# Attention stage of a two-layer model: weight loads in quarters, gathers on three units, two joins and one turn moved

## The chip, the cores and the metric

The kernel runs on one core of a Trainium2 chip. Its time is the device time in microseconds (us) of one execution. The core has five engines that run their own instruction queues: TensorE (PE in the profile; PEld is its weight load), VectorE (DVE), ScalarE (ACT), GpSimd (POOL) and SyncE (SP). SP only issues transfers here; 16 DMA engines carry them out. Engines wait for each other through semaphores.

## The reference

Four blocks, each added to a residual x of 4 x 512 rows of 512 numbers: a state-space block on a context, a mixture of experts, a cross-attention on the same context, and a ternary feed-forward. All in f32. The change touches the third block and the order of work around it:

```
x = x + _L0_xattn_ref(ctx_1024, _layernorm(x), ...)
x = x + _L0_ffn_ref(_layernorm(x), ...)
x = x + _L1_xattn_ref(_layernorm(x), ctx_1024, L1_xattn_Wq, L1_xattn_Wk, L1_xattn_Wv, L1_xattn_Wo, L1_xattn_gq, L1_xattn_gk)
x = x + _L1_ffn_ref(_layernorm(x), L1_ffn_w1, L1_ffn_w2)

def _L1_xattn_ref(hidden_states, encoder_hidden_states, Wq, Wk, Wv, Wo, gq, gk):
    q = (hidden_states @ Wq).reshape(B, Sq, H, D)
    k = (encoder_hidden_states @ Wk).reshape(B, Skv, H, D)
    v = (encoder_hidden_states @ Wv).reshape(B, Skv, H, D)
    q = rmsnorm(q, gq)
    k = rmsnorm(k, gk)
    scores = jnp.einsum('bqhd,bkhd->bhqk', q, k) * scale
    attn = jax.nn.softmax(scores, axis=-1)
    out = jnp.einsum('bhqk,bkhd->bqhd', attn, v)
    return out.reshape(B, Sq, H * D) @ Wo
```

Here there are 4 batches of 512 queries and 512 keys, 16 heads of 128.

## The kernel before

The last function, `attend`, holds the attention, and between its steps the end of the expert block (gathers of expert rows and their sum), the layer norms and the feed-forward of the batch before. Keys and values were computed earlier and lie in device memory.

**Tiling.** A *group* is four heads of one batch (16 groups, `groups`; 64 heads, `heads`). A head's 512 queries are taken in four *quarters* of 128 rows (`KB` is 4). One step of the main loop, a *unit* u = 4 n + i, belongs to quarter i of head n. Quarters go through five steps that are spread over units:

- `scores(n, i)`: one matmul into a PSUM bank (two banks), VectorE takes each row's maximum (L1958), ScalarE the exponential and the row's sum (L1961). The result, e, has three buffers.
- `weights(n, i)`, one unit later: VectorE's reciprocal (L1966) and scaling of e (L1967).
- The scaled quarter is turned, in one of two ways. `turn`: four transposes on TensorE into PSUM (`pet`, L2020) and a copy by ScalarE (L2021). Or by DMA: `split` takes the two 16-bit halves apart into `planes` (ScalarE L1985, GpSimd L1986), SP issues a DMA transpose (L1988) into `turned`, and two units later `join` copies the halves together into `eT` (VectorE L1995, ScalarE L1996). `by_dma` says which: from head 4 on the first three quarters go by DMA, and the fourth by TensorE; the last head goes by TensorE altogether.
- `values(n)`, at the third unit (i = 2) of head n + 1: four matmuls (`po`, L2027), once all four quarters are in `eT`.
- `project`: the product with Wo for one of the four row blocks (`px`, L2036), a group later.

The queries of the next group are projected meanwhile, one row block per head: `queries` (L1921) at i = 1, then ScalarE's square (L1924), `norm_q` at i = 2, `scale_q` at i = 3, and the turn of the normed queries, by DMA for the first three blocks (`split_q`, `join_q`), by TensorE for the fourth (`turn_q`). Groups 1 to 14 do this (56 heads); group 0's and group 1's queries are projected ahead of the loop, and group 15 has none to project.

**The order** is written out by hand. Each engine runs its instructions in program order, so a step that waits holds up everything behind it on its engine, and SP's queue holds the loads and the transposes of all heads in one line. In each unit the loop calls the steps of attention, then the list `front` (steps that begin with a matmul), then `weights` and `split`, then the list `back`. The steps that the change touches stand in the lists like this, with u the first unit of a head:

```
        if h == 0:
            put(back, u, load_q, j + 2)
            put(back, u + 1, load_o, b, g)
...
            for k in range(3):
                if 0 <= 3 * (at - 2) + k < NC * TOPK:
                    put(back, u + k, add, 1)
            if 0 <= 3 * (at - 1) < NC * TOPK:
                put(back, u + 2, fetch, min(3, NC * TOPK - 3 * (at - 1)))
```

`load_q` loads a group's 512 columns of Wq, `load_o` its 512 rows of Wo, 1 MB each, once per group. `fetch` issues gathers of one expert's row for 128 tokens each (`yg`, L1845, an indirect DMA issued by GpSimd, four buffers); `add` sums them into x on VectorE (L1853). In the first three batches heads 1 to 11 of the batch fetch.

**Queues around the steps.** On SP, one head's line is: transposes of quarters 0, 1 and 2, the loads of a later head's keys, key scales and values (`load_kv`), the transpose of the queries. On GpSimd, a head's line is: planes of quarters 0 and 1, two small steps of `norm_q` (L1932, L1933), the three gathers, planes of quarter 2, the scaling of a later head's keys (L1913), planes of the queries. The feed-forward's steps of the batch before stand between these from batch 1 on.

The last keys (batches 2 and 3) are still computed before the loop; `key_row` gives the buffers for their squares and for the keys, both from the seven buffers `oT`.

Of the kernel before, what the change touches and what calls it, by code (L numbers as in the profile page):

```python
# [17 lines left out]
F32 = mybir.dt.float32  # L18
# [12 lines left out]
P = 128  # L31
B, S, DM = 4, 512, 512
NT = B * S // P
NC = DM // P
# [4 lines left out]
E, TOPK, SEL, FI = 64, 8, 4, 192  # L39
# [19 lines left out]
HG = 4  # L59
# [1126 lines left out]
class Keys:  # L1186
# [4 lines left out]
    KB = S // P  # L1191
# [622 lines left out]
def attend(ctx, cm, x_all, w, kv, y_dram, wk, pos, tern, late, ctx_k, wk_k, out):  # L1814
# [5 lines left out]
    tc, nc = cm.tc, cm.nc  # L1820
    pool = {n: ctx.enter_context(tc.tile_pool(name=f"c_p{n}", bufs=n)) for n in (1, 2, 3, 4, 7)}
# [5 lines left out]
    W4 = HG * HD  # L1827
    KB = S // P
# [4 lines left out]
    heads = [(b, g, h) for b, g in groups for h in range(HG)]  # L1833
    xnTs, st = {}, {}
# [45 lines left out]
        nc.scalar.copy(xnTs[t], pt)  # L1880


    def load_q(j):
        if j < len(groups):
            b, g = groups[j]
            s = st[b, g] = {}
            s["Wq"] = pool[2].tile([P, NC, W4], F32, name="Wq")
            nc.sync.dma_start(s["Wq"], w["Wq"][:, g * W4:(g + 1) * W4].rearrange(
                "(c p) e -> p c e", p=P))

    def load_o(b, g):
        s = st[b, g]
        s["Wo"] = pool[2].tile([P, HG, DM], F32, name="Wo")
        nc.sync.dma_start(s["Wo"], w["Wo"][g * W4:(g + 1) * W4, :].rearrange("(h p) e -> p h e",
                                                                             p=P))

    def load_kv(n):
        if n < len(heads):
# [52 lines left out]
    def scores(n, i):  # L1951

        b, g, h = heads[n]
        pscore = psc.tile([P, S], F32, name="psc")
        nc.tensor.matmul(pscore, st[b, g]["qT"][:, h, i * P:(i + 1) * P], ks[n],  # L1955
                         start=True, stop=True)
        mx = small.tile([P, 1], F32, name="mx")
        nc.vector.tensor_reduce(mx, pscore, AX.X, ALU.max, negate=True)  # L1958
        e = pool[3].tile([P, S], F32, name="e")
        tot = small.tile([P, 1], F32, name="tot")  # L1960
        nc.scalar.activation(e, pscore, AF.Exp, bias=mx, accum_out=tot)  # L1961
        es[n, i] = e, tot

    def weights(n, i):
        e, tot = es[n, i]
        nc.vector.reciprocal(tot, tot)  # L1966
        nc.vector.tensor_scalar(e, e, tot, None, ALU.mult)  # L1967

    planes, turned = {}, {}

    def by_dma(n, i):
        if not HG <= n < len(heads) - 1:
            return False
        return i < 3

    def split(n, i):

        e, _ = es.pop((n, i))
        turned[n, i] = turn_planes(e[:, :])

    def turn_planes(e):

        halves = e.bitcast(I16).rearrange("p (s two) -> p two s", two=2)
        t = pool[2].tile([P, 2, S], I16, name="planes")
        nc.scalar.copy(t[:, 1], halves[:, 1])  # L1985
        nc.gpsimd.tensor_copy(t[:, 0], halves[:, 0])  # L1986
        out = pool[3].tile([P, 2 * KB, P], I16, name="turned")
        nc.sync.dma_start_transpose(out, t.rearrange("p two s -> p (two s)"))  # L1988
        return out

    def join_planes(out, t, i):

        out = out.bitcast(I16).rearrange("p k (s two) -> p two k s", two=2)
        at = slice(i * P, (i + 1) * P)
        nc.vector.tensor_copy(out[:, 1, :, at], t[:, KB:])  # L1995
        nc.scalar.copy(out[:, 0, :, at], t[:, 0:KB])  # L1996

    def join(n, i):

        if n not in eTs:  # L2000
            eTs[n] = pool[1].tile([P, KB, S], F32, name="eT")
        join_planes(eTs[n][:, :, :], turned.pop((n, i)), i)
# [11 lines left out]
    def turn(n, i):  # L2014
        if n not in eTs:
            eTs[n] = pool[1].tile([P, KB, S], F32, name="eT")
        e, _ = es.pop((n, i))
        pt = ptr.tile([P, KB, P], F32, name="pet", tag="pt")
        for kc in range(KB):
            nc.tensor.transpose(pt[:, kc, :], e[:, kc * P:(kc + 1) * P], cm.ident)  # L2020
        nc.scalar.copy(eTs[n][:, :, i * P:(i + 1) * P], pt)  # L2021

    def values(n):
        po = pav.tile([HD, S], F32, name="po")
        eT, v = eTs.pop(n), vs.pop(n)
        for kc in range(KB):
            nc.tensor.matmul(po, v[:, kc, :], eT[:, kc, :], start=kc == 0, stop=kc == KB - 1)  # L2027
        oTs[n] = pool[7].tile([HD, S], F32, name="oT")
        nc.scalar.copy(oTs[n], po)
# [122 lines left out]
    front, back = {}, {}  # L2152

    def put(where, u, f, *a):
        where.setdefault(u, []).append((f, *a))

    last = len(groups) - 1
    for n, (b, g, h) in enumerate(heads):
        j = n // HG
        u = n * KB  # L2160
        if j < last and j > 0:
            after = groups[j + 1]
            put(front, u + 1, queries, *after, h)
            put(back, u + 2, norm_q, *after)
            put(back, u + 3, scale_q, *after)
            if h < HG - 1:
                put(back, u + 4, split_q, *after, h)
                put(back, u + 6, join_q, *after, h)
        if j > 0:
            put(front, u + 4, project, j - 1, h)  # L2170
        if j < last and j > 0 and h == HG - 1:
            put(front, u + 4, turn_q, *groups[j + 1], h)
        if j > 0:
            put(back, u + 5, take_projected, j - 1, h)
        if h == 0:
            put(back, u, load_q, j + 2)
            put(back, u + 1, load_o, b, g)
        put(back, u + 3, load_kv, n + 3)
        put(back, u + 3, norm_k, n + 2)
        at = n % H  # L2180
        if b + 1 < B:
            for k in range(3):
                if 0 <= 3 * (at - 2) + k < NC * TOPK:
                    put(back, u + k, add, 1)
            if 0 <= 3 * (at - 1) < NC * TOPK:
                put(back, u + 2, fetch, min(3, NC * TOPK - 3 * (at - 1)))
            if at >= 11 and at < 15:
                t = (b + 1) * NC + at - 11
                put(back, u + 1, stats, t, "c")
                put(back, u + 3, normed, t, "c")  # L2190
                put(front, u + 4, turn_x, t)
        if b > 0 and h == 1:
            t = (b - 1) * NC + g
            put(back, u + 2, stats, t, "d")
            put(back, u + 4, ffn_x, t)
            put(back, u + 5, ffn_xq, t)
            put(front, u + 6, ffn_xT, t)

            put(front, u + 7, ffn_up, t, 0)
            put(front, u + 11, ffn_up, t, 1)  # L2200
            for k, at in enumerate((8, 9, 12, 12)):
                put(back, u + at, ffn_max, t, k)
            put(back, u + 12, ffn_h, t)
            for k in range(4):
                put(back, u + 13 + k // 2, ffn_hq, t, k)
            put(front, u + 14, ffn_hT, t, 0)
            put(front, u + 15, ffn_hT, t, 1)
            put(front, u + 15, ffn_down, t, 0)
            put(front, u + 19, ffn_down, t, 1)
            put(back, u + 20, ffn_y, t)  # L2210
            put(back, u + 20, store, t)

    def do(where, u):
        for f, *a in where.pop(u, []):
            f(*a)
# [5 lines left out]

    def key_row(n):

        return pool[7].tile([P, S], F32, name=f"k_{n}", tag="oT")

    def key_bank(shape, name):
        if name == "kpss":
            return pav.tile(shape, F32, name=name, tag="po")
        return psc.tile(shape, F32, name=name, tag="psc")

    keys = Keys(cm, w, kv, small, key_row, key_bank,
                lambda b: (ctx_k[b], 0), direct=ms)
    keys.wk = wk_k
# [13 lines left out]
    for n in range(NC * TOPK):  # L2247
        at = n % 16 - KB
        if n >= 16 and 0 <= at < KB:
            at = -1  # L2250
# [22 lines left out]
    for i in range(NC):  # L2273
# [3 lines left out]
        at = FRONT + i * WINDOW  # L2277
# [18 lines left out]
    for f, n, time in ((load_q, 0, 9.5), (load_kv, 0, 14.5), (load_q, 1, 17.5), (load_kv, 1, 44),  # L2296
                       (load_kv, 2, 50)):
        later(time, f, n)
# [17 lines left out]
    for *_, f, a in sorted(steps, key=lambda x: x[:2]):  # L2316
        f(*a)
    assert not left
    load_q(2)
    load_o(0, 0)  # L2320
    load_kv(3)
    put(back, KB * 3 + 4, last_norms)
# [3 lines left out]
    for u in range(KB, len(heads) * KB + 2):  # L2326
        n, i = divmod(u, KB)
        if n < len(heads):
            scores(n, i)
        if i == 2:  # L2330
            values(n - 1)
        if not by_dma(*divmod(u - 2, KB)):
            turn(*divmod(u - 2, KB))
        if by_dma(*divmod(u - 3, KB)):
            join(*divmod(u - 3, KB))
        do(front, u)
        if n < len(heads):
            weights(*divmod(u - 1, KB))
            if by_dma(*divmod(u - 1, KB)):
                split(*divmod(u - 1, KB))  # L2340
        do(back, u)
        if u == len(heads) * KB:
            weights(*divmod(u - 1, KB))
# [124 lines left out]
```

## Time and profile before

| | us |
|---|---|
| runs shown: median of 3 | 2537.57 |
| lowest and highest | 2534.87, 2537.62 |
| the profiled execution | 2537.26 |
| its span, first to last instruction | 2535.3 |
| TensorE busy in the span | 2367.0 |
| VectorE, ScalarE, GpSimd busy | 1585.2, 1362.9, 1333.4 |
| window 1470 to 2400: TensorE busy of 930 | 893.32 |
| window 2400 to 2535: TensorE busy of 135 | 112.03 |

The state-space block fills about the first 600 us, the experts run to about 1370, the attention with the feed-forward inside to about 2466, and the last batch's feed-forward ends the span. The profile comes from one execution. A line of its groups or waits names the source line (L1967 is line 1967 of the kernel), the engine, what is written and read, and how often. A "wait" is idle time of an engine in front of an instruction, with what ended it. "Granted clock" is the share of TensorE's clock that the chip let through in that stretch; "DMA share" is the mean busy share of the 16 DMA engines.

### The profile page before, as it was taken

The numbers are of one execution on the slowest core, as the hardware profiler recorded it, in microseconds if no ns is written. First come the engines' busy times: TensorE is split into PE (matmuls) and PEld (weight loads), VectorE is DVE, ScalarE is ACT, GpSimd is POOL, SyncE is SP. The second block draws the span as 40 slices with busy tenths as digits, with TensorE's granted clock in tenths as the row PEclk, the third lists the DMA queues.
The fourth block names the chain that finished last, engine by engine and source line by source line (L and its number), as shares of the span: only waits on it lengthen the run. The fifth ranks groups of instructions, "written<-read, shape, count | busy, mean of one in ns | idle before, by whom it ended". The sixth has DMA issues, their size and how long they took to land. (4 is left out here: it accounts for less than half of the span.)

```text
span 2535.3 us, 29085 instructions
## 1 busy us (share of the span) xinstructions
PE 2367.0 (93%) x9051; PEld 1289.9 (51%) x9051; DVE 1585.2 (63%) x2784; ACT 1362.9 (54%) x2554; POOL 1333.4 (53%) x1327
## 2 busy tenths in 40 slices
PE   6989899988999999999998988999999999999987
PEld 2555555655556566667664433444444444444443
DVE  6999998946332443344324565667776787666646
ACT  6777777755222222232323455666667666766753
POOL 7999999930443444444325344445553565333312
PEclk8999999989999999999998999999999999999999
DMA  5362636242766677899856467678876887666630
GB/s 207 96 217 79 224 109 209 96 162 99 232 213 206 204 231 235 282 314 340 269 186 217 151 171 176 168 172 192 191 172 151 191 198 179 144 142 136 139 77 21
DMA packets 445378, 456.17 MB, mean 180 GB/s; under 512 B 280756, under 2 KB 321796, under 8 KB 441121
## 3 DMA queue, kind: packets, MB, share of 16 engines
q1 hardware_dynamic: 401758, 297.86, 42.3%
q0 software_dynamic: 41408, 156.20, 20.0%
q8 instruction: 74, 1.21, 0.2%
q14 instruction: 88, 0.71, 0.1%
q10 hardware_dynamic: 2050, 0.18, 0.1%
HBM read 312.18 MB, written 79.82 MB: 155 GB/s over the span
## 5 line engine op out<-in xcount | busy, mean ns | idle before, releaser
L1315 PE MATMUL pg<-xT,wg 128*128 128x284 f32 (+12 forms) x1536 | 393.7, 400 | 1.8 <-ACT h L1326 0.7
L1986 POOL COPY planes<-e 128x512 int16<-128x512 int16 x177 | 117.0, 661 | 456.4 <-DVE e L1967 246.1
L1315 PEld LDWEIGHTS pg<-xT,wg 128*128 128x128 f32 x1536 | 278.6, 191 | 91.7 <-issue 41.8
L493 POOL TENSOR_TENSOR dBu<-bb,du 128x1024 f32<-128x1024 f32 x128 | 303.3, 2391 | 4.0 <-DVE dA L518 3.4
L1958 DVE TENSOR_REDUCE mx<-psc 128x1 f32<-128x512 f32 x256 | 175.9, 687 | 203.9 <-PE psc L1955 201.3
L1256 POOL DMA_INDIRECT xg<-xn_dram,tok x168 | 174.2, 1037 | 202.7 <-PE pt L1299 147.7
L1961 ACT ACTIVATE e<-psc,mx 128x512 f32<-128x512 f32 x256 | 176.4, 689 | 165.4 <-DVE mx L1958 160.6
L1955 PE MATMUL psc<-kT,qT 128*128 128x512 f32 x512 | 260.0, 594 | 0.2 <-ACT e L1961 0.2
L2027 PE MATMUL po<-eT,v 128*128 128x512 f32 x512 | 232.0, 596 | 13.8 <-ACT eT L1996 10.1
L1921 PE MATMUL pq<-Wq,xnT 128*128 128x512 f32 x512 | 233.9, 600 | 2.6 <-ACT xnT L1880 1.5
L2036 PE MATMUL px<-Wo,oT 128*128 128x512 f32 x512 | 230.9, 594 | 0.5 <-DVE qn L1939 0.5
L504 ACT ACTIVATE dA<-delta,negA 128x512 f32<-128x512 f32 x256 | 176.5, 695 | 52.0 <-DVE hc L519 31.6
L518 DVE TENSOR_TENSOR_SCAN dA<-dA,dBu 128x1024 f32<-128x1024 f32 x80 | 186.5, 2331 | 16.3 <-ACT dA L504 6.5
L1360 DVE COPY yo<-po 128x512 f32<-128x512 f32 x68 | 46.9, 691 | 197.9 <-PE po L1349 197.9
L2027 PEld LDWEIGHTS po<-eT,v 128*128 128x128 f32 x512 | 95.8, 190 | 141.7 <-issue 113.6
L2036 PEld LDWEIGHTS px<-Wo,oT 128*128 128x128 f32 x512 | 95.9, 190 | 123.7 <-issue 105.2
L524 PEld LDWEIGHTS yT<-ident,hc 128*128 128x128 f32 x1024 | 118.0, 143 | 78.5 <-issue 44.7
L1360 ACT COPY yo<-po 128x512 f32<-128x512 f32 (+3 forms) x64 | 37.5, 587 | 222.9 <-PE po L1349 215.9
L1256 POOL DMA_INDIRECT wd<-down,widx x64 | 62.9, 982 | 176.5 <-PE po L1349 163.1
L524 PE MATMUL yT<-ident,hc 128*128 128x128 f32 x1024 | 132.0, 276 | 20.7 <-DVE yg L558 9.7
L1967 DVE TENSOR_SCALAR e<-e,tot 128x512 f32<-128x512 f32 x256 | 141.3, 552 | 13.7
L1996 ACT COPY eT<-turned 128x512 int16<-128x512 int16 x177 | 135.6, 766 | 23.2 <-DMA turned<-planes 23.2
(367 smaller groups left out, 4613.0 us busy)
## 6 DMA issues: line engine op xcount, KB each, us to landing
y_dram<-yo SPq DMA_DIRECT2D x110, 256.0 KB
bb<-bc_dram SPq DMA_DIRECT2D x16, 1024.0 KB
cb<-bc_dram SPq DMA_DIRECT2D x16, 1024.0 KB
v_dram<-v SPq DMA_DIRECT2D x64, 256.0 KB
k_dram<-k_kT SPq DMA_DIRECT2D x64, 256.0 KB
Wq<-Wq SPq DMA_DIRECT2D x16, 1024.0 KB
kT<-k_dram SPq DMA_DIRECT2D x64, 256.0 KB
rk<-r_dram SPq DMA_DIRECT2D x64, 256.0 KB
```

What stands on the lines that cost most here:

```text
L493: nc.gpsimd.tensor_tensor(dBus[q], st[b]["bb"][i // 2][:, j:j + 2, :], st[b]["du"][c].unsqueeze(1).to_broadcast([P, 2, S]), ALU.mult)
L504: nc.scalar.activation(dAs[q][:, j, :], st[b]["delta"][c], AF.Exp, scale=negA[:, c, n:n + 1])
L518: nc.vector.tensor_tensor_scan(*flat, 0.0, ALU.mult, ALU.add)
L524: nc.tensor.matmul(yT[:, lc, :], t[:, lc * P:(lc + 1) * P], cm.ident, is_transpose=True, start=first and lc == 0, stop=last, skip_group_ch ...
L1256: nc.gpsimd.indirect_dma_start(out=t[0:n, :], out_offset=None, in_=table, in_offset=bass.IndirectOffsetOnAxis(ap=index, axis=0))
L1315: nc.tensor.matmul(pg[:, 0:n], s["wg"][:, c, m * P:(m + 1) * P], s["xT"][:, c, 0:n], start=c == 0, stop=c == NC - 1)
L1921: nc.tensor.matmul(pq.rearrange("p h d -> p (h d)"), xnTs[b * NC + i][:, c, :], s["Wq"][:, c, :], start=c == 0, stop=c == NC - 1)
L1955: nc.tensor.matmul(pscore, st[b, g]["qT"][:, h, i * P:(i + 1) * P], ks[n], start=True, stop=True)
L1958: nc.vector.tensor_reduce(mx, pscore, AX.X, ALU.max, negate=True)
L1961: nc.scalar.activation(e, pscore, AF.Exp, bias=mx, accum_out=tot)
L2027: nc.tensor.matmul(po, v[:, kc, :], eT[:, kc, :], start=kc == 0, stop=kc == KB - 1)
L2036: nc.tensor.matmul(px, oTs[j * HG + h][:, i * P:(i + 1) * P], st[b, g]["Wo"][:, h, :], start=h == 0, stop=h == HG - 1)
```

## The change

- Wq and Wo are loaded in four quarters of 256 KB, one in each head of a group, in place of one load of 1 MB at the group's first head.
- The three gathers of a head are issued at its first, second and fourth unit, one each, in place of all three at its third.
- Heads 60 to 62 turn their third quarter on TensorE.
- The joins of quarters 0 and 1 (at i = 3 and i = 0) stand behind `weights` and `split` of their unit; the join of quarter 2 (at i = 1) stays in front.
- The fourth quarter's turn (at i = 1) stands behind `front`, which holds the queries' projections.
- The squares of the last keys take their row from the two buffers `planes`.

```
-    def load_q(j):
+    def load_q(j, c0=0, c1=NC):
         if j < len(groups):
             b, g = groups[j]
-            s = st[b, g] = {}
-            s["Wq"] = pool[2].tile([P, NC, W4], F32, name="Wq")
-            nc.sync.dma_start(s["Wq"], w["Wq"][:, g * W4:(g + 1) * W4].rearrange(
-                "(c p) e -> p c e", p=P))
-
-    def load_o(b, g):
+            if c0 == 0:
+                st[b, g] = dict(Wq=pool[2].tile([P, NC, W4], F32, name="Wq"))
+            nc.sync.dma_start(st[b, g]["Wq"][:, c0:c1, :],
+                              w["Wq"][c0 * P:c1 * P, g * W4:(g + 1) * W4].rearrange(
+                                  "(c p) e -> p c e", p=P))
+
+    def load_o(b, g, h0=0, h1=HG):
         s = st[b, g]
-        s["Wo"] = pool[2].tile([P, HG, DM], F32, name="Wo")
-        nc.sync.dma_start(s["Wo"], w["Wo"][g * W4:(g + 1) * W4, :].rearrange("(h p) e -> p h e",
-                                                                             p=P))
+        if h0 == 0:
+            s["Wo"] = pool[2].tile([P, HG, DM], F32, name="Wo")
+        nc.sync.dma_start(s["Wo"][:, h0:h1, :],
+                          w["Wo"][g * W4 + h0 * P:g * W4 + h1 * P, :].rearrange(
+                              "(h p) e -> p h e", p=P))
...
         if not HG <= n < len(heads) - 1:
             return False
-        return i < 3
+        return i < (3 if n < len(heads) - HG else 2)
...
-        if h == 0:
-            put(back, u, load_q, j + 2)
-            put(back, u + 1, load_o, b, g)
+        if j > 0:
+            put(back, u, load_q, j + 2, h, h + 1)
+            put(back, u + 1, load_o, b, g, h, h + 1)
...
-            if 0 <= 3 * (at - 1) < NC * TOPK:
-                put(back, u + 2, fetch, min(3, NC * TOPK - 3 * (at - 1)))
+            for k in range(3):
+                if 0 <= 3 * (at - 1) + k < NC * TOPK:
+                    put(back, u + (0, 1, 3)[k], fetch, 1)
...
     def key_row(n):
 
+        if n == "sq":
+            return pool[2].tile([P, S], F32, name="k_sq", tag="planes")
         return pool[7].tile([P, S], F32, name=f"k_{n}", tag="oT")
...
-        if not by_dma(*divmod(u - 2, KB)):
-            turn(*divmod(u - 2, KB))
-        if by_dma(*divmod(u - 3, KB)):
-            join(*divmod(u - 3, KB))
+        before, landed = divmod(u - 2, KB), divmod(u - 3, KB)
+        if not by_dma(*before) and i != 1:
+            turn(*before)
+        if by_dma(*landed) and i == 1:
+            join(*landed)
         do(front, u)
+        if not by_dma(*before) and i == 1:
+            turn(*before)
         if n < len(heads):
             weights(*divmod(u - 1, KB))
             if by_dma(*divmod(u - 1, KB)):
                 split(*divmod(u - 1, KB))
+        if by_dma(*landed) and i != 1:
+            join(*landed)
         do(back, u)
```

## The prediction

> **What bounds the kernel now.** I read the busy time by stage first, then the attention stage's groups, then TensorE's waits, then two heads in order of time. Attention runs from about 1440 to 2466 us. The windows give busy time of PE, PEld, DVE, ACT, POOL, then granted clock, DMA share and GB/s:
>
> ```profile
> 1440.00:1640.00 200.00, 178.69 (x482) 81.59 (x483) 128.89 (x271) 113.83 (x234) 90.03 (x108) 0.97 0.72 182
> 1640.00:2420.00 780.00, 758.93 (x2196) 343.56 (x2194) 559.10 (x1220) 527.57 (x986) 365.28 (x473) 1.00 0.73 167
> 1557.00:1575.00 18.00, 16.02 (x38) 7.46 (x39) 10.90 (x24) 9.74 (x20) 8.58 (x11) 0.91 0.55 125
> ```
>
> TensorE is the bound: 97% busy over 780 us, every other engine under 72%. An edit that only moves work is worth at most TensorE's idle time, 21 us in each of the first two rows. Its waits there (waiter, releaser, us in total, times, longest), 1440 to 1640 and then 1640 to 2420:
>
> ```profile
> PE pet L2020 <- DVE e L1967: 17.7, 12, 6.0
> PE po L2027 <- ACT eT L2021: 3.1, 4, 1.0
> PE pet L2020 <- ACT qT L1949: 0.7, 1, 0.7
> ```
>
> ```profile
> PE po L2027 <- ACT eT L1996: 5.6, 7, 1.8
> PE pet L2020 <- DVE e L1967: 4.5, 5, 1.3
> PE ph L2105 <- DMA Tx<-xq: 4.0, 7, 1.0
> ...
> PE pet L2020 <- ACT qT L1949: 1.6, 2, 0.8
> ```
>
> The turn of a head's fourth quarter (pet) waits most, for the scaling of e; then the values (po), for a join's copy. One head in order of time, start and duration first:
>
> ```profile
> 1568.16 1.16 POOL L1845 DMA_INDIRECT yg<-y_dram,pos  x1 [0.20 <-issue]
> ...
> 1571.82 0.62 POOL L1986 COPY planes<-e 128x512 int16<-128x512 int16 x1
> ...
> 1573.49 0.50 DVE L1995 COPY eT<-turned 128x512 int16<-128x512 int16 x1 [2.55 <-DMA turned<-planes]
> ...
> 1574.07 0.67 DVE L1967 TENSOR_SCALAR e<-e,tot 128x512 f32<-128x512 f32 x1
> ...
> 1574.79 0.66 PE L2020 MATMUL pet<-ident,e 128*128 128x128 f32 x4 [1.55 <-DVE e L1967]
> ...
> 1575.29 3.60 PE L1921 MATMUL pq<-Wq,xnT 128*128 128x512 f32 x8
> ...
> 1578.72 1.02 PE L1955 MATMUL psc<-kT,qT 128*128 128x512 f32 x2
> ...
> 1578.92 0.60 ACT L1924 ACTIVATE sq<-pq 128x512 f32<-128x512 f32 x1 [0.88 <-PE pq L1921]
> ...
> 1579.58 3.60 PE L2027 MATMUL po<-eT,v 128*128 128x512 f32 x8
> ```
>
> VectorE idled 2.55 us at a join whose transpose had not landed; the scaling stood behind that join, and the turn behind the scaling, so TensorE lost 1.55 us. In heads 5 to 11, where each head issues three gathers, such a wait comes every head; the head of 1640 us issues none and has none. After the longest wait, 5.96 us at 1557.43, the clock of the next stretch is 0.91 (third window).
>
> **Part by part.** The profiled execution took 2537.26 us, of which the span is 2535.3; the median of the runs shown is 2537.57, 0.3 above it. I sum against 2537.26.
>
> *Joins behind the scaling, and the turn behind the queries' projections.* Either alone takes away most of the pet waits. In the head shown the exponentials' sum is read by 1572.11, so the scaling, no longer behind the join, ends at about 1572.9 (0.15 + 0.5 and the hops), before the turn is due at 1573.24; the projections in front of the turn give 3.43 us more (1575.29 to 1578.72). The 5.96 us wait needs the first part, since 3.43 alone would leave 2.5. The pet waits sum to 17.7 + 0.7 + 4.5 + 1.6 = 24.5, less 0.8 in group 0, where no projections run: **-23.7**. The clock after the two longest waits returns too: the eight matmuls behind 1557.43 took 4.47 us to the next start against 3.43, and the turn 0.88 against 0.44; behind 1487.63 the projections took 5.12: 1.5 + 1.7 = **-3.2**.
>
> What stands behind the moved instructions: a waiting join now holds the adds and the next row maximum on VectorE, the fourth part's planes and the next exponential on ScalarE. From the landing at 1573.49: join 0.45, add 0.74, maximum 0.69, exponential and its read 0.9, the second join 0.5, so about 1576.8. The projections would end at 1576.7. The cover is therefore just used up: each us by which a transpose lands later is a us of wait at the values.
>
> What is late next is the turn's copy. On ScalarE it now stands behind the square, which waits for all projections. Worked from the turn's start: square at +0.20, copy at +0.70 (the square holds ScalarE 0.5), 0.58 long, values released at +1.32. TensorE gets there at 0.44 + 0.86 = +1.30. So it is late by 0.03, and a waiting first weight load costs another 0.10 (1701.65 to 1705.18 is 3.53 against 3.43): 0.13 per head. Bounds: 0 (no wait in the head shown), and 0.97 from group 0, where turn, scores and values already follow each other:
>
> ```profile
> 1459.22 1.02 PE L1955 MATMUL psc<-kT,qT 128*128 128x512 f32 x2
> ...
> 1460.59 0.58 ACT L2021 COPY eT<-pet 128x512 f32<-128x512 f32 x1
> ...
> 1461.21 1.12 PE L2027 MATMUL po<-eT,v 128*128 128x512 f32 x2 [0.97 <-ACT eT L2021]
> ```
>
> There the copy stands behind an exponential issued in the same unit; here 3.43 us of projections cover that exponential, so I take 0.13: 56 heads, **+7** (0 to +54).
>
> *Gathers spread.* The count stays three per head, 0.95 to 1.16 us each on GpSimd. Back to back they hold it from 1568.16 to 1571.81, while the scaled e was ready at 1569.74: the planes copy came 2.1 us late, and its transpose with it. One at a time they hold a copy at most 1.2 us. The statistics of the feed-forward stand behind the same gathers (rstd, wanted at about 1830.2, came at 1831.3; VectorE idled 1.17 there, and the maximum, the exponential and the values were late in turn). Of the 5.6 us of po waits for joins, 1.76 belong to head 59, where nothing changes; most of the rest has this cause: **-4** with a little of the 4.0 at the feed-forward's input. Bounds 0 and -8.
>
> *Loads in quarters.* 13 loads of Wq and 15 of Wo become 112, 84 more issues on SP at 0.4 to 0.6 us: some 40 us of SP, about 0.7 per head. The transposes are queued behind them. SP stands 478.6 us waiting for ScalarE's plane copies in this stage, which covers it; without that cover a transpose would start 0.7 us later and, by the chain above, the values with it. Bytes and packets (2048 B) are the same. They no longer come as 2 MB in one head: 1537 to 1557 had a DMA share of 1.02 and the longest wait behind it. But heads 5 to 11, at 0.73, each get 512 KB more; 2048-byte packets take 90 to 120 ns, 256 of them over 16 engines 1.7 us, so a 14.4 us head would be (11.7 + 1.7)/14.4 = 0.93 full. I charge **+2** (0 to +11, a wait of 1.55 in each of seven heads as now).
>
> The Trainium skill speaks against this edit: "DMA: Bandwidth & Descriptors", section "Bandwidth", says to batch to 1 MiB or more, and its fit of 2.0 us plus bytes over 436 GB/s makes an estimate of 4.4 us for one load and 10.4 for four quarters. If that showed in full on TensorE it would be 28 times 6, 168 us; no run here shows quarter loads of these weights yet.
>
> *Two joins fewer in the last group.* Heads 60 to 62 turn their third quarter on TensorE: 3 x 4 transposes, 3 x 0.44 = 1.3, and each may wait for its scaling (0.17 to 0.5, group 0's rows and the order of work). Gone are waits of 1.52, 1.61 and 1.30 at the values; the 0.97 of group 0 stays in their place, so 1.5 is gained: **+1** (-3 to +3).
>
> *The square's row among the planes.* Only the last keys use it, before 1440; its two buffers follow each other as far as the evictions do: 0, bounds -1.3 and +1.3 (k_sq idled 1.3 for kpss).
>
> Sum: -23.7 - 3.2 + 7 - 4 + 2 + 1 = -20.9, so 2516.4 us. **Forecast 2516.5**, its own range 2510 to 2524 (the 0.13 between 0 and 0.27).
>
> **Rivals.**
> A, *better*: the copy is in time everywhere and the last group's waits go whole: -23.7 - 3.2 - 8 + 2 = -33, 2504. For it: the 0.03 is within what modelled matmul ends can tell. Against: the 0.10 comes with any lateness.
> B, *transposes become the limit*: in the gathers' heads the engines are 0.93 full and the join keeps 1.55 per head, now at the values; with seven heads in batch 0 and half as many with less in the later ones, some 15 us come back: 2531. For it: the cover of the chain above is nil. Against: the third transpose starts 2 us earlier.
> C, *slower, the copy behind the square*: the wait of group 0, 0.97, stands in all 56 heads: +54 in place of +7, 2537.3 - 27.9 + 54 = 2563. The break-even is 27.9/56 = 0.50 us per head, just the time the square holds ScalarE. For it: ten of 56 squares begin 0.5 to 1.5 us late already (at 1701, 1836, 1972 and others). Against: most of those stand behind the blocked GpSimd.
> D, *no change*: the waits move one for one from pet to po, within 5 us of 2537.6. For it: both depend on the same transposes.
>
> **Chances.** Forecast 0.50, A 0.12, B 0.14, C 0.14, D 0.10. The 0.2% that such a measurement can tell is 5 us, so faster 0.76, same 0.10, slower 0.14. The range takes in A and B and half of D: 2503 to 2540, leaving out C and little else.
>
> **What would show it.** Right: PE pet without DVE e among TensorE's waits; a new row po from ACT eT L2021's counterpart of some 7 us; windows of 200 us from 1440 with 190 or more busy and the clock at 1.00; projections right behind the scores at every head; heads 5 to 11 at 14.5 us in place of 16. Wrong: po waits above 25 us (C if the releaser is the turn's copy, B if the join's copy or the transposes), Wq or Wo among TensorE's releasers, or transposes that land more than 6 us after their issue.

## The result, and the profile after

The changed kernel is slower by 0.32%: a ratio of 1.0032 to the kernel before, 95% interval 1.002 to 1.0043 (medians 2543.86 and 2535.86 us of 22 runs each). Forecast was 2516.5.

The span of one execution also holds the stages ahead of the attention, whose clock differs between executions (see the last section). So I compare the attention by itself: the time between the copies of the values' results of two heads (`oT`, L2029 before, L2032 after). Head 1 to head 63 took 1011.9 us before and 1016.6 after, +4.6.

| heads | before | after | |
|---|---|---|---|
| 1 to 15: batch 0, no feed-forward inside | 219.5 | 200.8 | -18.7 |
| 15 to 47: gathers and feed-forward | 540.5 | 560.4 | +19.9 |
| 47 to 59: feed-forward, no gathers | 194.6 | 198.3 | +3.7 |
| 59 to 63 | 57.3 | 57.1 | -0.2 |

The gain came where it was forecast, in batch 0, and was given back later. The same two windows of the changed kernel (busy time of PE, PEld, DVE, ACT, POOL, clock, DMA share, GB/s):

```profile
1440.00:1640.00 200.00, 195.57 (x535) 88.69 (x534) 142.29 (x294) 125.05 (x258) 102.27 (x120) 1.00 0.77 191
1640.00:2420.00 780.00, 748.73 (x2138) 333.86 (x2137) 535.28 (x1190) 515.00 (x957) 356.22 (x459) 0.98 0.73 162
```

In the first TensorE is 17 us busier than before and at full clock; in the second it is 10 us less busy and the clock is lower. TensorE's waits in the second window (waiter, releaser, total, times, longest):

```profile
PE ph L2108 <- DMA Tx<-xq: 22.4, 11, 4.7
PE po L2030 <- ACT eT L2024: 5.0, 4, 2.2
PE pf L2143 <- ACT Th L2073: 2.5, 11, 0.2
PE pq L1924 <- ACT xnT L1880: 1.4, 2, 0.7
```

The turn (pet) is gone from the list. In its place stands the first matmul of the feed-forward (ph), which waits for `Tx`, the DMA transpose of its quantized input. That row was 4.0 us before. Batch 0, where there is no feed-forward, shows what the change does when nothing else is in the way. One head of it in TensorE's order of time:

```profile
1553.86 1.02 PE L1958 MATMUL psc<-kT,qT 128*128 128x512 f32 x2
1554.71 3.60 PE L1924 MATMUL pq<-Wq,xnT 128*128 128x512 f32 x8
1558.15 0.60 PE L2023 MATMUL pet<-ident,e 128*128 128x128 f32 x4
1558.58 1.02 PE L1958 MATMUL psc<-kT,qT 128*128 128x512 f32 x2
1559.47 3.70 PE L2030 MATMUL po<-eT,v 128*128 128x512 f32 x8
```

No wait is named anywhere; the values start 0.89 after the scores, where 0.86 is the unhindered step, and take 3.70 where 3.60 is usual. That is the forecast 0.13 per head, and the head takes 14.31 us.

Now the first head with a feed-forward, SP, GpSimd and TensorE of the changed kernel in order of time:

```profile
1679.24 1.24 SPq L1991 DMA_TRANSPOSE turned<-planes  x1
1679.53 0.99 POOL L1845 DMA_INDIRECT yg<-y_dram,pos  x1 [0.17 <-issue]
1680.54 0.57 SPq L1896 DMA_DIRECT2D Wo<-Wo  x1
1681.22 1.19 SPq L2068 DMA_TRANSPOSE Tx<-xq  x1
1682.25 1.02 PE L1958 MATMUL psc<-kT,qT 128*128 128x512 f32 x2
...
1687.20 3.59 PE L2108 MATMUL ph<-w,Tx 128*128 128x512 fp8e4 x8 [3.93 <-DMA Tx<-xq]
...
1690.58 1.91 PE L1958 MATMUL psc<-kT,qT 128*128 128x512 f32 x2
```

and the same place before the change:

```profile
1702.62 1.23 SPq L1988 DMA_TRANSPOSE turned<-planes  x1
1703.90 1.28 SPq L2065 DMA_TRANSPOSE Tx<-xq  x1
1705.18 1.02 PE L1955 MATMUL psc<-kT,qT 128*128 128x512 f32 x2
...
1707.16 1.90 PE L2105 MATMUL ph<-w,Tx 128*128 128x512 fp8e4 x8 [0.96 <-DMA Tx<-xq]
```

Before, `Tx` followed the transpose of quarter 0 directly and was used 3.3 us after its issue. Now a gather and a quarter of Wo stand right in front of it, and it is used 6.0 us after its issue. TensorE idles 3.93 us, and then the eight matmuls take 3.59 us where they took 1.90, the scores 1.91 where 1.02: the clock has halved. The DMA packets on record show the order: the 64 packets of the gather (4096 bytes each) ended at 1684.08, the 128 of Wo's quarter (2048 bytes each, issued at 1680.54) ran from 1683.54 to 1684.66, and `Tx`, behind Wo in SP's queue, was used at 1687.20. Between heads 15 and 47 the records hold 23.9 us of half clock, before the change none.

### The profile page after: what moved, and what is told of

Read it like the earlier page. It is cut to its first block, busy times and chain, and to the rows that moved or that the text cites. A ratio compares the mean times of both kernels' runs of the same rounds, so it can differ in the third digit from the quotient of the medians.

```text
span 2538.0 us, 29323 instructions
## 1 busy us (share of the span) xinstructions
PE 2370.1 (93%) x9063; PEld 1285.5 (51%) x9063; DVE 1577.0 (62%) x2781; ACT 1361.4 (54%) x2551; POOL 1334.6 (53%) x1324
## 3 DMA queue, kind: packets, MB, share of 16 engines
q0 software_dynamic: 41408, 156.20, 20.1%
## 5 line engine op out<-in xcount | busy, mean ns | idle before, releaser
L2030 PE MATMUL po<-eT,v 128*128 128x512 f32 x512 | 238.5, 609 | 11.5 <-ACT eT L2024 10.5
L518 DVE TENSOR_TENSOR_SCAN dA<-dA,dBu 128x1024 f32<-128x1024 f32 x80 | 186.0, 2324 | 15.6 <-POOL x_all L560 6.7
L1924 PEld LDWEIGHTS pq<-Wq,xnT 128*128 128x128 f32 x512 | 96.1, 190 | 127.7 <-issue 110.2
L1845 POOL DMA_INDIRECT yg<-y_dram,pos x108 | 115.9, 1073 | 60.5 <-DMA y_dram<-yo 33.7
```

The lines of the kernel that those rows point to most:

```text
L518: nc.vector.tensor_tensor_scan(*flat, 0.0, ALU.mult, ALU.add)
L1924: nc.tensor.matmul(pq.rearrange("p h d -> p (h d)"), xnTs[b * NC + i][:, c, :], s["Wq"][:, c, :], start=c == 0, stop=c == NC - 1)
```

## The experiments

Twelve kernels. A ratio is to the kernel before in the same session, with its 95% interval. The columns of heads are us in one profile each; "ph" is TensorE's wait for `Tx` between heads 1 and 63, "half" the time at half clock there. e9 and e14 run the same code up to head 59 and differ by 3.1 us on the way there, so a difference of that size in the columns tells nothing.

| kernel | ratio | 1-15 | 15-47 | 47-59 | 59-63 | 1-63 | ph | half |
|---|---|---|---|---|---|---|---|---|
| before | 1 | 219.5 | 540.5 | 194.6 | 57.3 | 1011.9 | 4.0 | 10.2 |
| changed | 1.0032 (1.002-1.0043) | 200.8 | 560.4 | 198.3 | 57.1 | 1016.6 | 23.3 | 23.9 |
| e1_reorder_only | 0.9951 (0.9933-0.9969) | 212.7 | 536.2 | 195.9 | 57.0 | 1001.8 | 2.5 | 6.8 |
| e5_loads_only | 1.0015 (0.9997-1.0033) | 211.8 | 550.2 | 197.3 | 58.1 | 1017.3 | 20.1 | 13.7 |
| e6_gathers_only | 0.9938 (0.9914-0.9961) | 203.7 | 542.4 | 194.6 | 58.0 | 998.7 | 11.8 | 6.8 |
| e2_gathers_together | 0.998 (0.9965-0.9995) | 206.4 | 547.5 | 198.6 | 57.1 | 1009.5 | 15.6 | 10.2 |
| e3_whole_loads | 0.9956 (0.9942-0.997) | 201.8 | 545.7 | 195.8 | 56.0 | 999.4 | 12.1 | 6.8 |
| e13_wo_moved | 0.9961 (0.9944-0.9977) | 200.8 | 549.5 | 195.8 | 56.1 | 1002.2 | 15.3 | 10.2 |
| e11_wq_quarters | 0.9949 (0.9932-0.9966) | 200.8 | 546.7 | 195.9 | 56.1 | 999.4 | 11.9 | 6.8 |
| e4_behind_tx | 0.9951 (0.9934-0.9968) | 204.0 | 547.3 | 195.8 | 56.1 | 1003.1 | 7.4 | 6.8 |
| e8_wo_behind_tx | 0.995 (0.9931-0.9969) | 204.3 | 540.6 | 195.8 | 56.1 | 996.8 | 6.1 | 0.0 |
| e9_whole_023 | 0.9927 (0.9903-0.9952) | 204.3 | 537.2 | 195.9 | 56.1 | 993.5 | 3.2 | 3.4 |
| e14_last_group | 0.9958 (0.9942-0.9974) | 205.3 | 539.3 | 195.9 | 57.0 | 997.5 | 5.4 | 3.4 |
| e12_by_batch | 0.9924 (0.9899-0.995) | 200.8 | 535.3 | 195.9 | 56.0 | 988.0 | 2.3 | 0.0 |

**One part alone.** e1: the loop of the changed kernel in the kernel before, nothing else.

```
-        if not by_dma(*divmod(u - 2, KB)):
-            turn(*divmod(u - 2, KB))
-        if by_dma(*divmod(u - 3, KB)):
-            join(*divmod(u - 3, KB))
+        before, landed = divmod(u - 2, KB), divmod(u - 3, KB)
+        if not by_dma(*before) and i != 1:
+            turn(*before)
+        if by_dma(*landed) and i == 1:
+            join(*landed)
...
+        if not by_dma(*before) and i == 1:
+            turn(*before)
...
+        if by_dma(*landed) and i != 1:
+            join(*landed)
```

> The kernel before with the new order of joins and turn alone: gathers together at i = 2, loads of 1 MB, last group and key rows as before. Three theories of why the changed kernel gives its 22 us back: G, the gather issued at i = 1, some 2 us ahead of the feed-forward's transpose Tx, shares the DMA engines with it; W, the quarter of Wo issued at i = 1 stands on SP between the transpose of quarter 0 and Tx; S, TensorE merely arrives earlier, since the pet wait that covered Tx is gone. G and W expect the pet waits gone (under 3 us), the ph waits for Tx at 4 to 8 us as before, and a time 15 to 25 us under the kernel before. S expects ph waits of 20 us or more and no gain.

S falls. The order alone keeps `Tx` on time and is faster, and still the pet waits are gone:

```profile
PE po L2027 <- ACT eT L2021: 16.5, 12, 7.3
PE pq L1921 <- ACT xnT L1880: 2.6, 4, 0.7
...
PE ph L2105 <- DMA Tx<-xq: 2.5, 3, 1.4
```

What remains is po, and 7.3 of its 16.5 us is one wait, at the values in head 9, behind the burst of 2 MB in head 8. A join on ScalarE idled 6.37 us for its transpose, and the turn's copy stands behind it. The burst does this only with the gathers together: e3 below, with the same loads and the gathers spread, has no wait over 1.2 us in batch 0. Batch 0 gets 6.8 of the 18.7 us. The expected size (15 to 25 us) was too high: 0.49% of 2532 is 12.

e5 and e6 are the kernel before with the quarter loads alone, and with the gathers at i = 0, 1, 3 alone:

```
+            put(back, u, load_q, j + 2, h, h + 1)
+            put(back, u + 1, load_o, b, g, h, h + 1)
```

```
+                    put(back, u + (0, 1, 3)[k], fetch, 1)
```

> The kernel before with the loads in quarters alone. Theory: the bursts behind heads 5 and 9 (waits of 3.3 and 5.96, and the halved clock behind them, some 9 us together) shrink to the 1.0 to 1.6 of the other heads, and each of the twelve Tx transposes is 0.7 to 1.1 us later, some 9 us: no change within 5 us, ph waits 11 to 16. Rival, that quarters cost by their number: more issues make all transposes later, pet waits grow over 30 us, slower by 10 us or more.

> The kernel before with the gathers spread over i = 0, 1 and 3 alone. Theory: the pet waits of 1.5 us in the gathers' heads shrink or go, since the third transpose starts 2 us earlier, and Tx waits 1.1 to 1.5 us longer in the heads with a gather in front of it (six or seven), ph waits 10 to 16; together faster by 0 to 10 us. Rival: the gathers' place does not matter for the pet waits, which stay at 20 us or more, and the time is the same or worse by the ph waits alone.

```profile
PE ph L2108 <- DMA Tx<-xq: 19.3, 11, 3.2
PE pet L2023 <- DVE e L1970: 12.6, 9, 2.1
```

```profile
PE ph L2105 <- DMA Tx<-xq: 10.9, 7, 2.4
PE pet L2020 <- DVE e L1967: 7.5, 7, 2.9
```

The first fence is e5 (1470 to 2400 us), the second e6. The kernel before had 21.4 for pet and 4.0 for ph there. The quarters do shrink the burst (pet's longest is 2.1, was 6.0; batch 0 gains 7.7), but they bring a `Tx` wait to nearly every feed-forward head, 0.9 to 3.2 us, in all 20.1 where 11 to 16 were expected: no gain. The gathers, spread, remove two thirds of the pet waits by themselves and delay `Tx` in the six heads where one stands in front of it; they are worth 0.6%, some 16 us where 0 to 10 were expected.

**One part undone.** e2 puts the gathers back together at i = 2; e3 puts back loads of 1 MB at the group's first head. Against the changed kernel, e2 first:

```
-                    put(back, u + (0, 1, 3)[k], fetch, 1)
+            if 0 <= 3 * (at - 1) < NC * TOPK:
+                put(back, u + 2, fetch, min(3, NC * TOPK - 3 * (at - 1)))
```

```
-        if j > 0:
-            put(back, u, load_q, j + 2, h, h + 1)
-            put(back, u + 1, load_o, b, g, h, h + 1)
+        if h == 0:
+            put(back, u, load_q, j + 2)
+            put(back, u + 1, load_o, b, g)
```

> The changed kernel with its three gathers together at i = 2 as before. G expects Tx to land 2.9 to 3.4 us after its issue in every head, the ph waits to fall from 26 to some 10 to 12 us, no halved clock between 1500 and 2400 us, and a time some 15 to 20 us under the changed kernel. W and S expect ph waits still above 20 us and a time within 5 us of the changed kernel.

> The changed kernel with loads of 1 MB at a group's first head. W expects Tx to be issued about 0.7 us earlier after its input, ph waits under 8 us in all, and a time 15 to 20 us under the changed kernel. G expects the ph waits of the heads with gathers to stay at 3 to 4 us, those of heads without gathers (0.8 to 1.1 each) to fall to 0.3 or less, and a time within 8 us of the changed kernel. If the quarters themselves earned part of the 22 us of batch 0, heads 8 to 10 get longer than their 14.3 us.

e2 first, then e3 (1470 to 2400 us):

```profile
PE ph L2108 <- DMA Tx<-xq: 14.7, 11, 4.1
```

```profile
PE ph L2108 <- DMA Tx<-xq: 12.0, 7, 5.1
```

Each takes ph to about half, and neither clears it: 15.6 and 12.1 of 23.3. G and W are both true. With the gathers together the waits are even, 0.7 to 1.2 us in most feed-forward heads: `Tx` is mostly issued 0.66 us after Wo's quarter and used 2.8 to 3.6 us after its issue, where 2.5 to 2.6 was usual before (3.3 in two heads). The longest, 4.09, is another case: there `Tx` itself was issued only after TensorE had come to want it (1825.78 against 1825.22). With whole loads the six heads that have no gather near `Tx` wait 0 to 0.5, those with a gather 1 us or so ahead of it 1.1 to 1.5, and once 5.05. In time, whole loads gain 17 us between heads 1 and 63 and the gathers' place 7. But the 7 is a balance: gathers together lose 5.6 us in batch 0 and gain 12.9 between heads 15 and 47, where whole loads gain 14.7. In batch 0 whole loads lose only 1.0 us, so the quarters hardly earned anything there. W alone had expected ph under 8 in e3, G alone 10 to 12 in e2: both missed.

e13 moves nothing but Wo's quarter, and e11 loads Wo whole and leaves Wq in quarters:

```
-            put(back, u + 1, load_o, b, g, h, h + 1)
+            put(back, u + 2, load_o, b, g, h, h + 1)
```

```
-            put(back, u + 1, load_o, b, g, h, h + 1)
+            if h == 0:
+                put(back, u + 1, load_o, b, g)
```

> The changed kernel with nothing but Wo's quarter moved from i = 1 to i = 2, behind Tx; gathers at i = 0, 1 and 3. W and G together expect ph waits near 12 (the gather's part stays: 1.0 to 1.8 in the six heads with a gather in front of Tx, nothing in the others), and head 1 to head 63 in 998 to 1004 us against 1016.6.

> The changed kernel with Wo loaded whole again and Wq still in quarters (Wq's quarter stands one unit earlier, ahead of the transpose of quarter 0, not between it and Tx). If Wo's place in front of Tx is what the quarters cost, ph waits fall from 23 to about 12, as with both loads whole, and head 1 to head 63 takes 998 to 1004 us. If any quarter load costs, it stays above 1008.

One step of Wo's quarter in SP's queue, from in front of `Tx` to behind it, is worth 14 us between heads 1 and 63, and takes the kernel from slower to faster than before. The ph waits fall by 8.0 us, and 13.7 us less run at half clock, which is worth at most half of that. The heads without gathers wait for `Tx` no longer than before the change (198.3 to 195.8 us from head 47 to 59, 2.2 of it this wait). Quarters of Wq, which stand a unit earlier, cost nothing that shows here: e11 equals e3 to 0.1 us and keeps batch 0 at 200.8. The ph wait in e13 came out at 15.3, not near 12:

```profile
PE ph L2108 <- DMA Tx<-xq: 15.3, 7, 3.9
```

**Both behind Tx.** e4 has gathers at i = 0, 2, 3 and Wo's quarter at i = 2; e8 gathers together and Wo's quarter at i = 2; e9 gathers at i = 0, 2, 3 and whole loads. e4 against the changed kernel:

```
-            put(back, u + 1, load_o, b, g, h, h + 1)
+            put(back, u + 2, load_o, b, g, h, h + 1)
-                    put(back, u + (0, 1, 3)[k], fetch, 1)
+                    put(back, u + (0, 2, 3)[k], fetch, 1)
```

e8 is the first of these two edits and that of e2, e9 the second and that of e3.

> The changed kernel with the second gather and the quarter of Wo moved from i = 1 to i = 2, behind Tx. G with W: Tx lands 2.5 to 3.3 us after its issue in all heads, ph waits under 8 us, the 22 us of batch 0 kept, time 2510 to 2520. S expects ph waits above 15 us still.

> The changed kernel with gathers together at i = 2, as in the run before of that name, and Wo's quarter moved from i = 1 to i = 2, behind Tx. W expects the 0.7 to 1.1 us of ph wait in each of the twelve feed-forward heads to go (14.7 down to 5 or less), Tx issued 0.7 us earlier against its input, and 8 to 12 us less than with the quarter in front of Tx, so 2515 to 2520. If the quarter's place is not the cause, ph waits stay at 12 us or more and the time within 4 us of that run.

> The changed kernel with loads of 1 MB at a group's first head, and the gathers at i = 0, 2 and 3. Against the run with whole loads and gathers at i = 0, 1, 3 only the gather's place in front of Tx differs. G expects its waits of 1.1 to 1.5 us (and 5.05 once) in the six heads with a gather in front of Tx to go, ph waits under 4 us in all, no halved clock between 1500 and 2400, time 2508 to 2518, the shortest so far. If sharing of the DMA engines is not the cause, ph waits stay near 12.

e8 against e2 confirms W (ph from 15.6 to 6.1, 13 us less; 3.49 of what is left is again the head in which `Tx` is issued late). e9 against e3 confirms G in the waits:

```profile
PE po L2030 <- ACT eT L2024: 8.5, 8, 2.0
PE ph L2108 <- DMA Tx<-xq: 3.1, 4, 1.2
```

That is e9, and 3.1 us is less than the 4.0 of the kernel before. In time e9 is 6 us shorter than e3; e14, the same code up to head 59, is 3 shorter without its 1 us in the last group, and the ratios do not tell the three apart. e4 still waits 1.9, 3.9 and 1.1 us in the first three feed-forward heads; there the quarter of Wq and the gather at i = 0, 4 to 8 us ahead, are still in the engines. In the second of these heads `Tx` was issued at 1747.99, while packets of the gather ran to 1751.74 and those of Wq's quarter to 1752.55. In the first two it takes both: e9 has this gather without the quarter and waits 0.46 and 0 there, e8 the quarter without the gather and waits 0.55 and 0.92.

**The last group, and a better kernel.** e14 is e9 with three quarters by DMA in heads 60 to 62 (`return i < 3` for `return i < (3 if n < len(heads) - HG else 2)`). e12 keeps the quarters and the gather at i = 1 where no feed-forward runs, in batch 0:

```
+        if j > 0 and b == 0:
+            put(back, u, load_q, j + 2, h, h + 1)
+            put(back, u + 1, load_o, b, g, h, h + 1)
+        elif b > 0 and h == 0:
+            put(back, u, load_q, j + 2)
+            put(back, u + 1, load_o, b, g)
...
+                    put(back, u + (0, 2 if b > 0 else 1, 3)[k], fetch, 1)
```

> The kernel with whole loads and gathers at i = 0, 2, 3, and the third quarters of heads 60 to 62 by DMA again. The prediction put the turn on TensorE at +1 us (-3 to +3). Against that kernel's 56.1 us from head 59 to head 63 this one should take 55.1 if the prediction was right, and 57.0 if the turn on TensorE gains what the profiles with three quarters by DMA suggest.

> The changed kernel with quarters and the gather at i = 1 only in batch 0, where there is no feed-forward and so no Tx; from batch 1 on loads of 1 MB and gathers at i = 0, 2, 3. Expected: heads 1 to 15 as in the changed kernel (201 us), heads 15 to 47 and 47 to 59 as with whole loads and gathers at 0, 2, 3 (537 and 196), together 990 us from head 1 to 63, 2 to 4 us less than the shortest so far; 0.991 to 0.993 of the kernel before.

In the last group, two quarters by DMA and two turns on TensorE are 1.0 us shorter than three and one (56.06 against 57.03). e12 is the shortest kernel of all by its heads, 988.0 us with no half clock and every wait short:

```profile
PE po L2030 <- ACT eT L2024: 5.6, 6, 1.7
PE pq L1924 <- ACT xnT L1880: 2.9, 6, 0.7
PE pf L2143 <- ACT Th L2073: 2.6, 11, 0.2
PE ph L2108 <- DMA Tx<-xq: 2.1, 3, 0.9
```

Its ratio, 0.9924, does not differ from e9's beyond their intervals.

## Why the prediction was wrong

- *What bounds the kernel, and the pet waits: right.* -23.7 was forecast and the waits between heads 4 and 59 are gone. Batch 0 became 18.7 us shorter, its heads 5 to 10 took 14.3 to 14.7 us each. The prediction's own terms for batch 0 make 19.4, by my estimate (17.6 of pet waits and 3.2 of clock, less 1.4 for the copy).
- *The turn's copy, +7: right where nothing else is late.* 0.13 per head stands in the record (0.03 and 0.10 in the head shown; 16.53 against 16.40 us in heads 47, 51 and 55). Between heads 15 and 47 it is about half of that: TensorE's busy time there is 525.5 us in e12, with no half clock, and 523.4 before, 2.0 more for 32 heads. Rival C, the copy behind the square, did not come.
- *Joins in the gathers' heads: right.* No wait of TensorE in batch 0 is put down to a join, and from 1486 to 1575 us TensorE was busy throughout, with a DMA share of 0.91, near the 0.93 worked out. Rival B did not come.
- *"Loads in quarters ... I charge +2": the step that failed.* I priced the queue only for the transposes of the quarters, "the transposes are queued behind them", and found cover for these in ScalarE's copies. `Tx` stands in the same queue, is issued 2 us before TensorE needs it, and had no cover: it already cost 4.0 us in the table that I read. I had not listed what follows Wo's quarter on SP. The term +2 measured 17 us between heads 1 and 63 (changed against e3), 14 of it by Wo's place alone (e13). One of the signs that the prediction gave for being wrong, a transpose more than 6 us after its issue, came at `Tx`: used 6.8 and 6.3 us after it in two heads.
- *"-4 with a little of the 4.0 at the feed-forward's input": the sign was wrong for the second half.* No wait is put down to a join's copy any more, but po's waits between heads 15 and 47 fell only from 3.9 to 3.2 us, so most of the -4 did not come. And the gather moved to i = 1 runs in front of `Tx`'s transfer. Against the place behind it, ph is 9 us longer (e3 against e9) and the time 3 to 6 us.
- *The clock.* I counted the halved clock as a gain of 3.2 in batch 0, and did not ask which new waits would be long enough to bring it back. From head 15 to 47 TensorE's idle time rose by 8.8 us (ph +16.4, pet -6.1, po -0.7, others -0.7) and its busy time by 11.1. e12, in the same order but with no half clock there, is busy 2.0 us more than before; so some 9 of the 19.9 us are the clock's.
- *The last group, +1: wrong sign, small.* -1.0 (e14); I had the values' wait left at 0.97, it was 0.77.
- *Not priced at all:* the turn used to stand between the transposes of the next batch's normed rows and the projections that use them, while ScalarE copied these rows. Now the projections come first and wait 0.11 to 0.69 us for that copy (pq). Heads 12 and 13 take 15.12 us where 14.61 was usual, 0.13 of it by the turn's copy.
- *Rival D, the waits move one for one*, was nearest, though its price, within 5 us of no change, was missed too: waits did move, but to another instruction than the one I named, and by another way, a queue.
- *What the Trainium skill said against small loads* ("DMA: Bandwidth & Descriptors", section "Bandwidth") spoke for whole loads, which did better from batch 1 on, but not by the price worked out from it. The page gives the fit behind that price for transfers that GpSimd issues, in another section; these loads are issued by SP. The estimate of 6 us per four quarters does not show: e11, with Wq in quarters, and e3, with whole loads, both take 999.4 us between heads 1 and 63. What cost was a place in a queue: that of Wo's quarters, and in e4 that of Wq's together with a gather.

Shown by the runs: both places in front of `Tx`, each by itself and together, and that the order of joins and turn is a gain by itself. With both placements undone, e9 takes 18.5 us less than the kernel before between heads 1 and 63, near the forecast 20.9; part of that is luck, since the -4 did not come and the copy cost less than its +7. The 0.32% of the result is 8 us, of which the profiles show 4.6 between heads 1 and 63; the rest cannot be told from the spread ahead of the attention, and the square's row among the planes, priced at 0, was not run by itself.

With the gather and Wo's quarter in front, `Tx` takes 3.4 to 6.8 us from issue to use; with the quarter alone in quiet heads 2.9 to 3.2, with the gather alone 3.6 to 4.7 (e6). The packets show Wo's quarter slowed by the gather: in the second feed-forward head its 128 packets took 244 ns each on average, beside the gather's, and 84 ns in the first, where they ran almost wholly behind them. Open is what each costs in one head: the gather alone led to 7.8 us once (e3), and e13, with Wo's quarter behind `Tx`, still takes 4.2 to 6.6 in the heads with gathers.

## What to carry to other kernels

When a transfer is moved in a queue, write down every later transfer of that queue that an engine waits for within the next few microseconds, and the slack of each, not only those that the change is about. The transfer with the least slack sets the price: here 256 KB placed one unit later was worth 14 us. Small waits on the bounding engine can cost less than one longer wait of the same sum, since the clock fell only behind stretches with about 2 us of idle time close together (next section).

## What the runs showed of the hardware

**The halved clock.** It comes in pieces of 3.4 and 6.8 us behind TensorE's waits. In the changed kernel, between heads 1 and 63, it came behind waits of 2.20, 2.77, 3.93, 4.35 and 4.74 us and not behind those of 1.75 or less; in e8 a wait of 3.49 left none. A window of the changed kernel, right behind the wait of 3.93 us, shows it:

```profile
1690.00:1696.00 6.00, 6.00 (x12) 2.68 (x11) 2.84 (x6) 4.51 (x8) 0.00 (x0) 0.74 0.59 153
```

TensorE is busy throughout at a granted clock of 0.74. The Trainium skill ("TensorE: Matmul & The Clock Gate", section "What's actually happening") has a free-running window of about 3.4 us, after an idle one of which the clock is halved. The records agree with the window: in all fourteen profiles every change of the clock lies a whole number of 3.413 us behind the first. But the window need not be idle throughout. Cut along that grid, from 1480 to 2440 us, the clock halved behind each of the 26 windows at full clock in which TensorE was idle for 1.99 us or more, and behind none of the 3877 with 1.93 us or less. So it matters where a wait falls: the 2.20 us lie within one window (2102.69 to 2106.11), and the 3.49 us of e8 are cut at 1831.29 into two parts of 1.75. By these figures, as an estimate, a single wait under 1.9 us leaves the clock alone, one over 4.0 always halves it, and between the two its place decides.

**The spread ahead of the attention.** Up to head 1 all these kernels run nearly the same instructions, yet head 1 came between 1443.6 and 1459.9 us, and the time at half clock up to there was 88.7 to 122.9 us. The two go together (a correlation of 0.86 over the fourteen profiles), and half of 34 us is of the size of the spread. But half clock is not all of it: with half of it taken off, head 1 still ranges over 11 us, and the earliest, e14, had 99.0 us of it. Part of a kernel is better compared by its own marks than by the span.
